# One product of each Strassen-Winograd projection split once more, and other places for the softmax weights

## The chip, the cores and the metric

The kernel runs on one core of one Trainium2 chip. The metric is the device time of one execution in microseconds, the median of several runs. Before the change it is 2482.03 us (three runs, 2481.46 to 2482.95).

A core has five engines, each with its own instruction queue that it works off in order: TensorE (PE; its weight loads are listed apart as PEld), VectorE (DVE), ScalarE (ACT), GpSimd (POOL) and SyncE (SP, which here issues the DMA transfers). They wait for each other through semaphores. Matmul results go to PSUM[...]; everything else lies in SBUF, 128 partitions wide.

## The reference

There are 128 graphs of 128 nodes with 512 features, float32, and two layers. Layer 0 reads them as batches, but its contractions are within one graph:

```
q, k, v = x @ Wq.T, x @ Wk.T, x @ Wv.T                  # layer 0
rel = adj.T * (q @ k.T);  rel = rel / norm(rel, rows)
x = layernorm(x + rel @ v)
q, k, v = x @ Wq + bq, x @ Wk + bk, x @ Wv + bv         # layer 1, 8 heads of 64
w = softmax(q @ k.T / 8 + mask(adj))                    # per head
x = layernorm(x + w @ v)
```

The kernel merges layer 0's two score weights into one matrix M (so y = x M stands for q and k together). That leaves five projections of 512 features to 512 features: m and v0 in layer 0, q, k and v1 in layer 1. They are most of the arithmetic.

## The kernel before, in words

**Tiling.** Four graphs make a group (512 tokens); there are 32 groups. Each projection of a group is a 512 x 512 by 512 x 512 product. It is done by one level of the Strassen-Winograd scheme: both operands are cut into quadrants of 256 x 256, and seven products P1 to P7 of quadrants, or of sums of quadrants, replace eight. The sums of the weights (`weight_sums`, tile `wc`) are made once, those of the tokens (`token_sums`, tiles `tx`) once a group, on VectorE and GpSimd. A product (`product`, L282) is four matmuls of 128 x 128 weights and 256 columns. A float32 matmul shows as two records, so a product shows as eight.

**A projection's course.** `Projection.step` takes the products in the order 1, 5, 6, 2, 3, 7, 4. P1, P6, P7 and P4 add up in one PSUM bank (`pa`), P5 and P3 in another (`pb`), P2 has one of its own (`pd`, from the pool `ps_m` of five banks that scores and outputs use too). ScalarE copies the running sums of P1, P5 and P6 out of the banks (`empty`, L290 or, with the bias, L293) into a tile `s`; VectorE adds the bank and one of these copies when P2, P3 and P7 are done (`add`, L297); ScalarE copies the last quadrant out after P4. A product that adds onto a bank waits until the copy before it has read that bank.

**The order of the work** is written out by hand. A round `r` has 35 slots. `dense` gives each slot one product; a projection starts every seven slots, and its P4 lies two slots inside the next projection. `short` holds all other steps, each with a slot number (halves allowed), in the tables `ZERO` (layer 0 of a group: scores, norm, outputs, layernorm, spill, staging, transposition), `STEADY`, `QUICK` and `LAST` (attention of layer 1). The loop at the end sorts the slots and issues what is in them; within an engine that is the order of execution. A slot number is no time: an instruction runs when its engine is free and its waits are over. In a steady round the projections are m and v0 of the next group, then q, k and v1 of this one.

**Other steps that are spoken of.** Layer 0's scores are `l0_score` (L334, 128-column matmuls; VectorE multiplies by the adjacency at L335, GpSimd squares at L336), its outputs `l0_out` (L379, L381). Layer 1's scores are `attn_scores` (L397, L401), then `attn_max`, `attn_exp` (ScalarE), a spill of the weights to DRAM and a staging back in an order that VectorE's 32 x 32 transposition needs, `attn_transpose`, `attn_out` (L450, L453), a way back through DRAM, and `attn_sum`, `attn_stats`, `attn_norm`. The last group has its own steps (`last_...`), without DRAM.

**Places.** SBUF tiles with one tag share a place in turn. Softmax weights `w` have two buffers of their own (tag "w"); layer 0's y and v have one place each ("yT", "v0"); the squares of layer 0 have one ("sq").

Of the kernel before, what the change touches and what calls it, by code (L numbers as in the profile page):

```python
# [18 lines left out]
def kernel(  # L19
# [15 lines left out]
    nc = tc.nc  # L35
# [101 lines left out]

    wc = {n: const.tile([P, 7, 2, HF], F32, name=f"wc_{n}") for n in ("m", "v0", "q", "k", "v1")}

    def weight_sums(t, a21, eng):  # L140
        eng.tensor_tensor(t[:, 4], a21, t[:, 3], op=ALU.add)
        eng.tensor_tensor(t[:, 5], t[:, 4], t[:, 0], op=ALU.subtract)
        eng.tensor_tensor(t[:, 6], t[:, 0], a21, op=ALU.subtract)
        eng.tensor_tensor(t[:, 2], t[:, 1], t[:, 5], op=ALU.subtract)
# [11 lines left out]
        return t.rearrange("p (q c r) -> p c q r", q=A, c=C)  # L156


    m21 = two.tile([P, 2, HF], F32, tag="w", name="m21")
    v21 = two.tile([P, 2, HF], F32, tag="w", name="v21")  # L160

    def layer0_weights():
        wq_p = one.tile([P, C, C, A, Q], F32, tag="v1", name="wq0_p")
# [24 lines left out]
        weight_sums(t, w[:, 0:2, HF:D], nc.gpsimd)  # L188


    XT, TX, YT, V0, REL, X1T, TX1, QT, KT, V1 = ({} for _ in range(10))
    SOFT = {}

    def transpose_quarter(dst, g, h, dh):
# [7 lines left out]
    def token_sums(t, xT, dh):  # L202

        if dh == 0:
            nc.vector.tensor_tensor(t[:, 0], quarter(xT, 0, 1), quarter(xT, 0, 0), op=ALU.subtract)
        else:
            nc.vector.tensor_tensor(t[:, 1], quarter(xT, 1, 1), t[:, 0], op=ALU.subtract)
            nc.gpsimd.tensor_tensor(t[:, 2], quarter(xT, 1, 1), quarter(xT, 0, 1), op=ALU.subtract)
            nc.gpsimd.tensor_tensor(t[:, 3], quarter(xT, 1, 0), t[:, 1], op=ALU.subtract)

    def x_transpose(g, dh, h):
        if dh == 0 and h == 0:
# [29 lines left out]
    class Projection:  # L242
# [7 lines left out]

        def begin(self):
            k, g = self.kind, self.g
            if k in ("m", "v0"):
                self.xT, self.t = XT[g], TX[g]
            else:
                self.xT, self.t = X1T[g], TX1[g]
            if k == "m":
                YT[g] = self.y = one.tile([P, C, G, P], F32, tag="yT", name=f"yT_{g}")
            elif k == "q":
                QT[g] = self.y = one.tile([P, C, G, P], F32, tag="qT" if g < NG - 1 else "yT", name=f"qT_{g}")  # L260
            elif k == "k":
                KT[g] = self.y = one.tile([P, C, G, P], F32, tag="kT", name=f"kT_{g}")
            elif k == "v0":
                V0[g] = self.y = one.tile([P, G, D], F32, tag="v0", name=f"v0_{g}")
            else:
                V1[g] = self.y = one.tile([P, G, D], F32, tag="v1" if g < NG - 1 else "v0", name=f"v1_{g}")
            self.s = one.tile([P, 3, 2, HF], F32, tag="s", name=f"s_{self.name}")

        def out(self, eh, th):
            if self.wide:  # L270
# [25 lines left out]
        def add(self, eh, th, bank, s):  # L296
            nc.vector.tensor_tensor(self.out(eh, th), bank, self.s[:, s], op=ALU.add)  # L297

        def step(self, i):
            if i == 1:  # L300
                self.begin()
                self.a = ps_a.tile([P, 2, HF], F32, tag="a", name=f"pa_{self.name}")
                self.product(1, self.a, True)
                self.empty(self.s[:, 0], self.a, 0)
            elif i == 5:
                self.b = ps_b.tile([P, 2, HF], F32, tag="b", name=f"pb_{self.name}")
                self.product(5, self.b, True)
                self.empty(self.s[:, 1], self.b, 1)
            elif i == 2:
                d = ps_m.tile([P, 2, HF], F32, tag="m", name=f"pd_{self.name}")  # L310
                self.product(2, d, True)
                self.add(0, 0, d, 0)
            elif i == 6:
                self.product(6, self.a, False)
                self.empty(self.s[:, 2], self.a, 0)
            elif i == 3:
                self.product(3, self.b, False)
                self.add(0, 1, self.b, 2)
            elif i == 7:
                self.product(7, self.a, False)  # L320
                self.add(1, 1, self.a, 1)
            elif i == 4:
                self.product(4, self.a, False)
                self.empty(self.out(1, 0), self.a, 1)

    def l0_score(g, b):

        if b == 0:
            REL[g] = (one.tile([P, G, P], F32, tag="rel", name=f"rel_{g}"),
                      one.tile([P, G, P], F32, tag="sq", name=f"sq_{g}"))  # L330
        rel, sq = REL[g]
        p = ps_m.tile([P, P], F32, tag="m", name=f"pst_{g}_{b}")
        for dc in range(C):
            nc.tensor.matmul(p, XT[g][:, dc, b, :], YT[g][:, dc, b, :], start=(dc == 0), stop=(dc == C - 1))  # L334
        nc.vector.tensor_tensor(rel[:, b], p, adj_sb, op=ALU.mult)  # L335
        nc.gpsimd.tensor_tensor(sq[:, b], rel[:, b], rel[:, b], op=ALU.mult)  # L336
# [51 lines left out]
    def l0_layernorm(g, b):  # L388
        normalized(graph(g, b), b, *RN[g])

    def attn_scores(g, b):

        p = [ps_m.tile([P, A, H // 2, Q], F32, tag="m", name=f"ps_{g}_{b}_{s}") for s in range(2)]
        for a in range(H // 2):
            for s in range(2):
                r = slice(s * HD, (s + 1) * HD)
                nc.tensor.matmul(p[s][:, :, a, :], QT[g][r, a, b, :], KT[g][r, a, b, :], start=True, stop=True)  # L397

        w = two.tile([P, 2, A, H // 2, Q], F32, tag="xl" if g == NG - 2 and b >= 2 else "w", name=f"w_{g}_{b}")
        for s in range(2):  # L400
            nc.vector.scalar_tensor_tensor(w[:, s].rearrange("p q a r -> p (q a r)"),  # L401
                                           p[s].rearrange("p q a r -> p (q a r)"), HD ** -0.5, mask,
                                           op0=ALU.mult, op1=ALU.add)
        nmax = small.tile([P, H], F32, tag="nmax", name=f"nmax_{g}_{b}")
        sums = small.tile([P, H], F32, tag="sums", name=f"sums_{g}_{b}")
        SOFT[g, b] = [w, nmax, sums]
# [97 lines left out]
    def last_scores(g, b):  # L504
        p = [ps_m.tile([P, H // 2, P], F32, tag="m", name=f"ps_{g}_{b}_{s}") for s in range(2)]
        for a in range(H // 2):
            for s in range(2):
                r = slice(s * HD, (s + 1) * HD)
                nc.tensor.matmul(p[s][:, a, :], QT[g][r, a, b, :], KT[g][r, a, b, :], start=True, stop=True)
        w = two.tile([P, H, P], F32, tag="w" if b < 2 else "xl", name=f"w_{g}_{b}")  # L510
        for s in range(2):
            nc.vector.scalar_tensor_tensor(w[:, s * (H // 2):(s + 1) * (H // 2)], p[s], HD ** -0.5,
                                           maskp[:, None, :].to_broadcast([P, H // 2, P]), op0=ALU.mult, op1=ALU.add)
# [57 lines left out]
    def last_store(g, b):  # L571
# [10 lines left out]

    ZERO = (
        ((18, 19, 20, 21), 22, (36, 36, 37, 37), 38, (39, 40), (40, 41), (42, 43), (46, 47, 49, 50)),
        ((10.5, 14, 10.5, 14), 15.5, (22, 22, 20.5, 18.5), 22.5, (24.5, 27), (32, 29.5), (33.5, 29.5), (36.5, 40.5, 41, 43.5)),
        ((11, 12, 13, 14), 16, (18, 19, 21, 22), 23, (24, 25), (25, 26), (26, 28), (31, 32, 33, 34)),
    )
    STEADY = (
        (32, (35.5, 35.5, 35.5, 35.5, 36), (35.5, 36), 39, (41.5, 51, 52, 53.5, 56.5, 59.5, 59.5, 61.5)),
        (32, (33.5, 37.5, 39, 41.5, 41.5), (42, 42), 42, (50, 51, 54.5, 60, 60.5, 63, 65.5, 72)),  # L590
        (51, (51.5, 51.5, 51.5, 53.5, 53.5), (52, 53.5), 56, (60, 67, 67, 68, 72, 74.5, 78, 78)),
        (51, (53, 54, 56, 56.5, 56.5), (56, 59), 61, (64.5, 67, 67.5, 74, 77, 81, 82, 84)),
    )
    QUICK = (
        (31.5, (32, 33.5, 34, 35, 35), (35, 37.5), 40.5, (44, 44, 44.5, 46.5, 50, 51.5, 51.5, 55)),
        (35.5, (36, 37, 37, 38, 38), (38, 41), 42.5, (44.5, 47.5, 48, 49.5, 52.5, 53.5, 58, 59.5)),
        (36, (39, 40, 41, 41, 41), (41.5, 42), 46, (49.5, 51.5, 51.5, 56.5, 56.5, 58.5, 61, 66.5)),
        (40.5, (41, 44, 45, 47, 47), (45, 49), 50, (54, 54.5, 59.5, 61, 62, 68, 68, 68)),
    )
    LAST = (  # L600
        (17, (17.5, 21.5), (22.5, 22.5), (24, 25), 29, 29, 29),
        (17.5, (18, 23), (24, 26.5), (28, 31), 36.5, 37, 37.5),
        (19, (23, 24.5), (27, 29.5), (31, 34.5), 41, 41, 42.5),
        (22.5, (25.5, 26), (29, 32), (34, 39), 41.5, 43.5, 47.5),
    )

    def at(r, k, f, *a):
# [2 lines left out]
    for r in range(-1, NG):  # L610
# [4 lines left out]
        for j, (kind, g) in enumerate(todo):  # L615
            if not 0 <= g < NG:
                continue
            pr = Projection(kind, g)
            for k, i in ((0, 1), (1, 5), (3, 6), (4, 2), (5, 3), (6, 7), (9, 4)):
                dense[R * r + 7 * j + k] = (pr, i)  # L620
    halves = [(dh, h) for dh in range(2) for h in range(2)]
    for g in range(NG):
# [11 lines left out]
        for i, (dh, h) in enumerate(halves):  # L634
            at(g - 2, ((24, 25, 27, 28) if g != 1 else (22, 23, 24, 25))[i], x_transpose, g, dh, h)
            at(g - 1, tr[i], x1_transpose, g, dh, h)
        for b in range(G):
            at(g - 1, sc[b], l0_score, g, b)
            at(g - 1, ou[b], l0_out, g, b)
# [29 lines left out]

    at(-1, 8, masks)  # L670
    at(-1, 41, layer1_weights, "k", "k")

    with tc.manual_schedule():
        layer0_weights()
# [39 lines left out]
```

## Time and profile before

| | |
|---|---|
| time, median of 3 | 2482.03 us |
| span of the profiled execution | 2480.6 us |
| TensorE busy | 2461.6 us |
| VectorE busy | 1603.6 us |
| ScalarE busy | 1012.8 us |
| GpSimd busy | 833.5 us |
| DMA moved | 404.73 MB |
| matmul records | 14656 |

Busy time is the sum of an engine's instructions without their overlaps. The durations of single records are from start to end; successive matmuls overlap, so what one costs is the distance between two starts. In a list of groups a row has the line, the engine, the operation, what it writes and reads with the shapes, how many there are, the busy time in us, the mean duration of one in ns, and the engine's idle time just before them with what ended it. In a list of waits a row has who waited for whom, the total in us, how often, and the longest.

### The profile page before, as it was taken

To read this page: it belongs to the slowest core of one execution; us is meant where nothing else is said; L and a number is where in the kernel's file an instruction comes from. 1 tells how busy PE (TensorE), PEld (TensorE's weight loads), DVE (VectorE), ACT (ScalarE), POOL (GpSimd) and SP (SyncE) were. 2 spreads that over 40 slices of the span, in tenths; PEclk is the share of its full clock that TensorE was granted. 3 is DMA by queue.
4 is the path that set the end of the run, shared out by engine and by line. 5 is a ranking of instruction groups with operands and counts; after the bars stand their busy time and mean duration, and the time that the engine had idled before them with its cause. 6 is when DMAs were issued, how large, how long until landed. Compare 5 with 4: busy or idle time off the path is not lost.

```text
span 2480.6 us, 41595 instructions
## 1 busy us (share of the span) xinstructions
PE 2461.6 (99%) x14656; PEld 2115.2 (85%) x14656; DVE 1603.6 (65%) x2715; ACT 1012.8 (41%) x3211; POOL 833.5 (34%) x1206
## 2 busy tenths in 40 slices
PE   8999999999999999999999999999999999999998
PEld 6888888888888888888888888888888888888886
DVE  5466676666666666666666666666666666666667
ACT  1243343433443433434334444434343344433454
POOL 3322333323323323233233233333332332323334
PEclk9999999999999999999999999999999999999999
DMA  7356656666555656556665556665566655665654
GB/s 158 102 132 166 179 154 166 169 164 170 173 159 160 176 164 183 156 160 169 169 170 170 157 160 175 162 183 159 162 171 164 174 166 157 165 175 159 182 149 141
DMA packets 508562, 404.73 MB, mean 163 GB/s; under 512 B 37569, under 2 KB 424769, under 8 KB 508353
## 3 DMA queue, kind: packets, MB, share of 16 engines
q1 hardware_dynamic: 508352, 402.08, 59.2%
q8 instruction: 114, 1.87, 0.3%
q14 instruction: 96, 0.78, 0.1%
HBM read 237.31 MB, written 164.63 MB: 162 GB/s over the span
## 4 chain that ended last, share of the span: by engine, by line
PE 98%; DVE 1%; issue 0%; DMA 0%; POOL 0%; POOLq 0%; ACT 0%; SPq 0%; DVEq 0%
PE pa_v L282 18%; PE pa_m L282 9%; PE pa_q L282 9%; PE pa_k L282 9%; PE pb_v L282 9%; PE ps L397 5%; PE po L450 5%; PE pd_v L282 5%; PE pst L334 5%; PE po L379 4%; PE pb_q L282 4%; PE pb_k L282 4%; PE pb_m L282 4%; PE pd_q L282 2%; PE pd_k L282 2%; PE pd_m L282 2%
## 5 line engine op out<-in xcount | busy, mean ns | idle before, releaser
L478 POOL TENSOR_TENSOR xr<-xr,bv_b 128x512 f32<-128x512 f32 x124 | 164.7, 1328 | 709.5 <-DMA xr<-x1d 300.6
L418 ACT ACTIVATE w<-w,nmax 128x128 f32<-128x128 f32 x992 | 384.8, 396 | 3.8 <-DVE nmax L411 3.8
L282 PE MATMUL pa_v<-wc_v,tx 128*128 128x256 f32 x1536 | 366.5, 382 | 0.0
L282 PEld LDWEIGHTS pa_v<-wc_v,tx 128*128 128x128 f32 x1536 | 289.6, 190 | 41.5 <-issue 0.6
L480 POOL TENSOR_TENSOR xr<-xr,o 128x512 f32<-128x512 f32 x124 | 157.4, 1269 | 288.6 <-issue 267.8
L418 ACT ACTIVATION_READ_ACCUMULATOR w<-w,nmax 128x1 f32 x992 | 193.6, 195 | 0.0
L282 PE MATMUL pa_m<-tx,wc_m 128*128 128x256 f32 x768 | 181.6, 380 | 0.8 <-DVE yT L297 0.8
L282 PE MATMUL pa_q<-tx,wc_q 128*128 128x256 f32 x768 | 181.7, 380 | 0.0
L282 PE MATMUL pa_k<-tx,wc_k 128*128 128x256 f32 x768 | 181.6, 380 | 0.0
L453 DVE STREAM_TRANSPOSE oT<-po 128x512 f32<-128x512 f32 x124 | 88.8, 716 | 141.2 <-PE po L450 139.9
L437 DVE STREAM_TRANSPOSE wT<-wl 128x1024 f32<-128x1024 f32 x124 | 153.8, 1240 | 30.2 <-DMA wl<-wd 30.2
L290 ACT COPY s_m<-pa_m 128x512 f32<-128x512 f32 x64 | 37.1, 580 | 330.6 <-PE pa_m L282 320.1
L290 ACT COPY s_v<-pa_v 128x512 f32<-128x512 f32 x128 | 74.9, 585 | 233.7 <-PE pa_v L282 233.7
L401 DVE SCALAR_TENSOR_TENSOR w<-ps,mask 128x512 f32<-128x512 f32 x248 | 154.2, 684 | 24.2 <-PE ps L397 24.2
L282 PEld LDWEIGHTS pa_m<-tx,wc_m 128*128 128x128 f32 x768 | 146.1, 190 | 21.1 <-DVE yT L297 1.2
L282 PEld LDWEIGHTS pa_k<-tx,wc_k 128*128 128x128 f32 x768 | 146.1, 190 | 19.7 <-issue 0.2
L282 PEld LDWEIGHTS pa_q<-tx,wc_q 128*128 128x128 f32 x768 | 146.0, 190 | 19.7 <-issue 0.2
L411 DVE TENSOR_REDUCE nmax<-w 128x4 f32<-128x512 f32 x248 | 154.8, 676 | 0.0
L374 ACT ACTIVATE xr<-xr,sh,rstd 128x512 f32<-128x512 f32 x124 | 100.8, 813 | 128.6 <-POOL sh L369 128.6
L196 DVE STREAM_TRANSPOSE x1T<-xl_h 128x512 f32<-128x512 f32 x128 | 90.1, 704 | 72.7 <-DMA xl_h<-x1d 72.7
L334 PEld LDWEIGHTS pst<-yT,xT 128*128 128x128 f32 x1024 | 124.7, 192 | 3.7 <-ACT yT L290 0.4
L397 PE MATMUL ps<-kT,qT 64*128 64x128 f32 x1984 | 127.7, 279 | 0.0
(160 smaller groups left out, 4905.6 us busy)
## 6 DMA issues: line engine op xcount, KB each, us to landing
wd<-w SPq DMA_DIRECT2D x248, 256.0 KB, 2.9
wl<-wd SPq DMA_DIRECT2D x496, 128.0 KB, 3.0
xl_x<-in_x_dram SPq DMA_DIRECT2D x256, 128.0 KB, 6.7
x<-in_x_dram SPq DMA_DIRECT2D x64, 512.0 KB, 5.6
x1d<-x SPq DMA_DIRECT2D x64, 512.0 KB, 2.9
xl_h<-x1d SPq DMA_DIRECT2D x256, 128.0 KB, 3.2
od<-oT SPq DMA_DIRECT2D x496, 64.0 KB, 1.9
o<-od SPq DMA_DIRECT2D x124, 256.0 KB, 3.1
```

What stands on the lines that cost most here:

```text
L282: nc.tensor.matmul(bank[:, m, :], l[:, k, m * P:(m + 1) * P], r[:, k, :], start=start and m == 0 and k == 0, stop=(m == 1 and k == 1), ski ...
L290: nc.scalar.copy(dst, bank)
L334: nc.tensor.matmul(p, XT[g][:, dc, b, :], YT[g][:, dc, b, :], start=(dc == 0), stop=(dc == C - 1))
L374: nc.scalar.activation(h, h, AF.Identity, bias=sh[:, b:b + 1], scale=rstd[:, b:b + 1])
L397: nc.tensor.matmul(p[s][:, :, a, :], QT[g][r, a, b, :], KT[g][r, a, b, :], start=True, stop=True)
L401: nc.vector.scalar_tensor_tensor(w[:, s].rearrange("p q a r -> p (q a r)"), p[s].rearrange("p q a r -> p (q a r)"), HD ** -0.5, mask, op0= ...
L411: nc.vector.tensor_reduce(nmax[:, s * (H // 2):(s + 1) * (H // 2)], w[:, s].rearrange("p q a r -> p a q r"), axis=AX.XY, op=ALU.max, negat ...
L418: nc.scalar.activation(w[:, s, :, a, :], w[:, s, :, a, :], AF.Exp, bias=nmax[:, i:i + 1], accum_out=sums[:, i:i + 1])
L437: nc.vector.transpose(wT, SOFT[g, b][0].rearrange("p a i r -> p i a r"))
L450: nc.tensor.matmul(p[s * HD:(s + 1) * HD, a, :], V1[g][:, b, h * HD:(h + 1) * HD], wT[:, s * (H // 2) + a].rearrange("p q t -> p (q t)"), ...
L478: nc.gpsimd.tensor_tensor(xr, xr, bv_b, op=ALU.add)
L480: nc.gpsimd.tensor_tensor(xr_, xr_, o, op=ALU.add)
```

## The change

P2 is the product of two plain quadrants of 256 x 256. The change applies the same scheme to it once more: seven products of 128 x 128 x 128 instead of four matmuls of 256 columns. Two quarters of P2's result need sums over several small products, and P2's result itself goes only to one quadrant of the output, onto P1's copy. The first group's m and v0 (`plain`) keep the old P2.

- New sums: of the weights once (`inner_weight_sums`, on GpSimd), of the tokens once a group and layer (`inner_token_sums`, on GpSimd, tiles `ux`).
- The small products come in four groups (`inner(0)` to `inner(3)`), placed by the table `INNER` between the products. They work in one bank of `ps_m` with three slots of 128 columns: three products, then two onto slots 0 and 1, then one onto slot 0, then one more onto slot 0. After each group VectorE adds the slots onto quarters of the output, which already hold P1's copy (`s0`). For v1, that copy lies in the place of layer 0's `rel`, and the output's place is taken later.
- The old P2 slot stays in the table, but is empty. So P3 follows P6.
- The memory for this comes from the softmax weights: a pair of them now lies in the place of layer 0's v or y, between uses. The squares lie in the place of `oT`.
- The tables ZERO, STEADY, QUICK and LAST have other slot numbers for many steps.

```diff
+    def inner_weight_sums(key, eng):
+        w = [None] + [inner_weight(key, i) for i in range(1, 8)]
+        eng.tensor_tensor(w[5], w[3], w[4], op=ALU.add)
+        eng.tensor_tensor(w[6], w[5], w[1], op=ALU.subtract)
+        eng.tensor_tensor(w[7], w[1], w[3], op=ALU.subtract)
+        eng.tensor_tensor(w[3], w[2], w[6], op=ALU.subtract)
...
+    def inner_token_sums(u, xT):
+
+        eng = nc.gpsimd
+        eng.tensor_tensor(u[:, 0], inner_token(xT, 5), inner_token(xT, 1), op=ALU.subtract)
+        eng.tensor_tensor(u[:, 1], inner_token(xT, 3), u[:, 0], op=ALU.subtract)
+        eng.tensor_tensor(u[:, 2], inner_token(xT, 3), inner_token(xT, 5), op=ALU.subtract)
+        eng.tensor_tensor(u[:, 3], inner_token(xT, 2), u[:, 1], op=ALU.subtract)
...
+        def inner_product(self, i, slot, start=False):
+            l, r = inner_weight(self.kind, i), self.u[:, {5: 0, 6: 1, 7: 2, 4: 3}[i]] if i >= 4 else inner_token(self.xT, i)
+        if self.wide:
+            l, r = r, l
+        nc.tensor.matmul(self.c[:, slot, :], l, r, start=start, stop=True, skip_group_check=True)
+
+        def inner(self, n):
+
+            add = nc.vector.tensor_tensor
+            self.u = (UX if self.kind in ("m", "v0") else UX1)[self.g]
+            if n == 0:
+                if self.kind == "v1":
+                    self.place()
+                self.c = ps_m.tile([P, 3, P], F32, tag="m", name=f"pc_{self.name}")
+                self.inner_product(1, 0, True)
+                self.inner_product(5, 1)
+                self.inner_product(2, 2)
+                y, s0 = self.quarters((1, 1))
+                add(y, self.c[:, 0:2], s0, op=ALU.add)
+                y, _ = self.quarters((0, 0))
+                add(y, self.c[:, 2], y, op=ALU.add)
+            elif n == 1:
+                self.inner_product(6, 0)
+                self.inner_product(3, 1)
+                y, s0 = self.quarters((0, 1))
+                add(y, self.c[:, 0], s0, op=ALU.add)
+                add(y, self.c[:, 1], y, op=ALU.add)
+            elif n == 2:
+                self.inner_product(7, 0)
+                y = self.last_quarter()
+                add(y, self.c[:, 0], y, op=ALU.add)
+            else:
+                self.inner_product(4, 0)
+                y, s0 = self.quarters((1, 0))
+                add(y, self.c[:, 0], s0, op=ALU.add)
...
             elif i == 2:
-                d = ps_m.tile([P, 2, HF], F32, tag="m", name=f"pd_{self.name}")
-                self.product(2, d, True)
-                self.add(0, 0, d, 0)
+                if self.plain:
+                    d = ps_m.tile([P, 2, HF], F32, tag="m", name=f"pd_{self.name}")
+                    self.product(2, d, True)
+                    nc.vector.tensor_tensor(self.s0, d, self.s0, op=ALU.add)
...
-                      one.tile([P, G, P], F32, tag="sq", name=f"sq_{g}"))
+                      two.tile([P, G, P], F32, tag="oT", name=f"sq_{g}"))
...
-        w = two.tile([P, 2, A, H // 2, Q], F32, tag="xl" if g == NG - 2 and b >= 2 else "w", name=f"w_{g}_{b}")
+        if g == NG - 2 and b >= 2:
+            w = two.tile([P, 2, A, H // 2, Q], F32, tag="xl", name=f"w_{g}_{b}")
+        else:
+            if b % 2 == 0:
+                WP[g, b // 2] = one.tile([P, 2, 2, A, H // 2, Q], F32, tag="yT" if b else "v0", name=f"w_{g}_{b}")
+            w = WP[g, b // 2][:, b % 2]
...
+    INNER = (
+        (2.71, 6.22, 8.23, 9.24),
+        (4.21, 8.72, 9.23, 9.74),
+        (2.21, 4.22, 6.73, 8.24),
+    )
...
-            for k, i in ((0, 1), (1, 5), (3, 6), (4, 2), (5, 3), (6, 7), (9, 4)):
+            for k, i in (*((0, 1), (1, 5), (3, 6), (4, 2), (5, 3), (6, 7), (9, 4)), *zip(INNER[2 if r == NG - 1 else kind == "v1"], range(10, 14))):
+                assert R * r + 7 * j + k not in dense
                 dense[R * r + 7 * j + k] = (pr, i)
```

The first row of `INNER` is for m, v0, q and k, the second for v1, the third for the last round. So, with the slots 0 (P1), 1 (P5), 3 (P6), 5 (P3), 6 (P7) and 9 (P4), and 7 and 8 for the next projection's P1 and P5, a projection other than v1 runs P1, P5, [the P4 before it], I0, P6, P3, P7, I1, next P1, next P5, I2, P4, I3; v1 has I0 ahead of P3, and I1, P4, I2, the next projection's I0, I3 at its end.

## The prediction

> **What bounds the kernel now.** I read the engines' busy time first, then the chain that ended last, then the waits of TensorE, and then its timeline.
>
> ```profile
> PE 2461.6 (99%) x14656; PEld 2115.2 (85%) x14656; DVE 1603.6 (65%) x2715; ACT 1012.8 (41%) x3211; POOL 833.5 (34%) x1206
> PEclk9999999999999999999999999999999999999999
> PE 98%; DVE 1%; issue 0%; DMA 0%; POOL 0%; POOLq 0%; ACT 0%; SPq 0%; DVEq 0%
> ```
>
> TensorE is busy for the whole span at full clock, and the chain is TensorE's own queue. Its waits add up to about 10 us, all in the first 55 us or the last 25:
>
> ```profile
> PE pM L177 <- DMA wk_s<-in_L_gnn_Wk_dram: 4.4, 1, 4.4
> PE po L546 <- DVE o L551: 1.8, 3, 1.2
> PE pa_m L282 <- DVE xT L196: 1.1, 1, 1.1
> PE pn L345 <- POOL sq L336: 0.9, 1, 0.9
> ```
>
> So between 55 and 2455 us a nanosecond off TensorE's queue is a nanosecond off the time, if no new wait appears; a nanosecond more on another engine costs nothing until TensorE waits for it. One steady round, from one pair of attention scores to the same pair of the next group, is 75.95 us, all TensorE (columns: length, PE, PEld, DVE, ACT, POOL, clock, DMA, GB/s):
>
> ```profile
> 1030.96:1106.91 75.95, 75.95 (x458) 65.57 (x458) 49.76 (x85) 31.47 (x100) 25.52 (x37) 1.00 0.61 167
> ```
>
> The prices of the two products stand side by side in TensorE's timeline:
>
> ```profile
> 1055.42 1.89 PE L282 MATMUL pa_v<-wc_v,tx 128*128 128x256 f32 x8
> 1057.15 1.95 PE L334 MATMUL pst<-yT,xT 128*128 128x128 f32 x16
> 1058.93 1.89 PE L282 MATMUL pd_v<-wc_v,xT 128*128 128x256 f32 x8
> 1060.66 1.89 PE L282 MATMUL pb_v<-wc_v,xT 128*128 128x256 f32 x8
> ```
>
> The reader should subtract starts, not read durations, which overlap. A product of L282 (four matmuls, eight records) takes 1058.93 to 1060.66, so 1.73 us, 0.216 a record. Sixteen records of 128 columns take 1057.15 to 1058.93, so 1.78 us, 0.111 a record, with the change of width into them and out of them included.
>
> **What the Trainium skill says.** "TensorE: Matmul & The Clock Gate", section "Wait — 56ns, not 53.3ns?": warm, matmuls follow each other at N/2.4 ns and about 2.5 ns more. The trace agrees if a float32 record streams its columns twice: 215.8 for 256 columns (0.216 here), 109.2 for 128 (0.111 here). The same page, "Step-by-step: what each phase is for", says that weight loads are pulled ahead of running matmuls. Here the 128-column loads of L334 have 190 to 193 ns each, yet records follow at 111, so they do overlap. "SBUF — State Buffer", "SBUF: two separate sides", says that a VectorE operation with two SBUF inputs and a GpSimd operation lock each other out. The added VectorE additions read one input from PSUM, so I don't count this; L297, of that kind, keeps its 691 ns.
>
> **The change part by part.** I call P2's seven small products by their groups: I0 (three products), I1 (two), I2 and I3 (one each).
>
> *TensorE.* Removed: P2, 1.726 us (eleven products from 1038.16 to 1057.15). Added: seven products of 128x128x128, two records each: 14 x 0.1113 = 1.558. Saved: 0.168 us a projection. There are 5 x 32 = 160 projections, and m and v0 of group 0 keep the old P2: 158 x 0.168 = **26.6 us**. The width changes cost nothing extra in the row above, even though the small products now come in groups of 6, 4, 2 and 2 records.
>
> *VectorE.* The kinds of operation, by their nearest rows:
>
> ```profile
> L335 DVE TENSOR_TENSOR rel<-pst,adj_sb 128x128 f32<-128x128 f32 x128 | 37.3, 292 | 98.2 <-PE pst L334 98.0
> L551 DVE TENSOR_TENSOR o<-po,rs 128x256 f32<-128x256 f32 x8 | 3.4, 425 | 2.0 <-PE po L546 1.3
> L297 DVE TENSOR_TENSOR v<-pd_v,s_v 128x512 f32<-128x512 f32 x64 | 44.2, 691 | 35.5 <-PE pd_v L282 35.5
> L336 POOL TENSOR_TENSOR sq<-rel 128x128 f32<-128x128 f32 x128 | 50.4, 398 | 152.5 <-DVE rel L335 151.7
> ```
>
> P2's addition (0.69) becomes one of 256 columns and five of 128: 0.425 + 5 x 0.292 = 1.89. That is 1.19 us more a projection, 158 x 1.19 = 188 us in all: VectorE goes from 1604 to about 1792 us, 73% of the new span; in a round 49.8 + 6.0 = 55.8 of about 75.1. It stays second. TensorE's products hide it, as long as each addition is done when its bank is written again.
>
> *GpSimd.* Four sums of 128 columns for each of 63 token tiles and five weights: 272 x 0.40 = 109 us, 833 to about 940, 38%. The token sums of a group are finished many products before their first use; hidden.
>
> *The new hand-offs.* I1, I2 and I3 reuse slot 0 of the bank and wait for the addition that read it; TensorE's whole queue stands behind such a wait. What one hand-off needs: the four-matmul score that starts at 1057.15 leaves the array after 8 x 0.111, at 1058.04, and its VectorE reader starts here:
>
> ```profile
> 1058.24 0.29 DVE L335 TENSOR_TENSOR rel<-pst,adj_sb 128x128 f32<-128x128 f32 x1 [1.44 <-PE pst L334]
> ```
>
> 0.20 to start, 0.29 for the addition, and 0.06 back (near the end L551 ends at 2460.27 and its waiter starts at 2460.33): 0.55 us, if VectorE is free. What lies between, from the slots: for m, v0, q and k, I1 to I2 has the next projection's P1 and P5 (3.45 us) and I2 to I3 has P4 (1.73): slack of 1.2 us or more, enough for one 1.15 us transposition in front. Laying VectorE's queue of a round against these places by the rows' durations, I find k the worst: some 3 us of backlog from transpositions and statistics before P3, and still I1's additions end 1.4 us before I2. For v1, I2 to I3 has only m's I0: six records, 0.67 us against 0.55. VectorE is idle there in this layout, so the wait is 0 to 0.1; it could be 0.6 if an operation of 512 columns got in front.
>
> *The other waits.* With P2 gone, only P3 (1.73 us) lies between P6 and P7, which writes P6's bank; before it was P2 and P3, 3.45. ScalarE needs 0.2 + 0.59 for a copy, or 0.2 + 0.84 for q's and k's two halves, and is 41% busy; four exps ahead of it (0.39 each, 1.55) would spoil it, but in q they are laid to end 1.8 us before P7 starts. Also, v0's bank is now held over the scores, so those work in four banks of the pool, not five; the last pair waits for the transposition of the output (0.64 after TensorE's end), which comes about level: 0 to 0.3. I take 0.1 us a round for these and v1 together: 31 x 0.1 = **3 us**; the bounds are 0 and 0.9 (28 us).
>
> *Softmax weights in the places of v and y.* No operation is added. Weights for graphs 0 and 1 lie in v's place from after its last reader until their spill; the next v writes graphs 2 and 3 some five products later. y's place is free from the last score (slot 11) to the next m (slot 35). A DMA read of some 3 us fits in both. Cost 0. The same goes for squares in oT.
>
> *Ends.* In the last 35 us VectorE, not TensorE, sets the pace: from 2442 to 2475 its operations stand nearly without a gap. The last v1's 1.19 us come on top: **+1.2**. At the start the first q may wait for its token sums, since four GpSimd sums follow the old ones: **+1**.
>
> Sum: 2482.0 - 26.6 + 3 + 1.2 + 1 = 2460.6; I say **2460**.
>
> **Rivals.** *A, nothing waits*: the bounds' low end, 2482 - 26.6 = 2455.4. For it: there is no steady wait now and every slack but one exceeds 0.5 us. Against: v1's 0.12 us. *B, hand-offs eat half*: v1's I3 and the fourth score bank late by some 0.45 us a round together, 14 us: 2471. For it: VectorE at 73% in strict order, where one late transfer (L196 waits 72.7 us for DMA now) holds up additions that TensorE now needs sooner. Against: those transfers get earlier places. *C, slower*: VectorE or ScalarE is late at every projection by more than the 0.168 saved; with 0.3 us each, 158 x (0.3 - 0.168) = +21, 2503. For it: three new TensorE waits a projection, 474 in all, and half the room before P7. Against: the round's VectorE sum, 55.8 of 75.1, and slack beyond 1 us at four of five. A version of C, where small matmuls can't hide their weight loads (14 x 0.19 = 2.66, +148 us), is refuted by the 0.111 of L334.
>
> **How the numbers follow.** Forecast 0.63, A 0.12, B 0.17, C 0.08, of which a part ends near no change. The low end takes in most of A; the high end reaches to B's value: 2454 to 2472. Faster by over 0.2% (under 2477): the forecast, A and B, 0.92; within it 0.03; slower 0.05.
>
> **What would show it.** Right: TensorE still at 98% or more, small products at 0.11 us a record, a round of about 75.2 us, VectorE near 1790, and waits of TensorE for VectorE of a few us in total. Wrong: a wait of TensorE for the additions of I2 or I1 some 31 or 158 times, or for ScalarE's copies before P7, or a gap at each change of width, which would bring the record over 0.111.

## The result and the profile after

The changed kernel takes 2458.86 us (median of 4 runs, 2458.22 to 2459.89), the kernel before 2481.79 beside it (2481.46 to 2482.95): ratio 0.9907, 95% interval 0.989 to 0.9924. The forecast was 2460, with a range of 2454 to 2472.

First the busy time, the clock and the chain on the page of the kernel after:

```profile
PE 2435.0 (99%) x15604; PEld 2123.7 (86%) x15604; DVE 1738.2 (71%) x3505; ACT 1000.4 (41%) x3211; POOL 952.3 (39%) x1478
PEclk9999999999999999999999999999999999999999
PE 98%; DVE 1%; POOL 0%; issue 0%; DMA 0%; POOLq 0%; ACT 0%; SPq 0%; DVEq 0%
```

TensorE has 948 records more and is busy 26.6 us less (2461.6 before). That this is the forecast's saving to the tenth is chance: up to 3.4 us of it come from two stretches of the trace of before that ran at half the granted clock (see the last section). The chain is still TensorE's own queue. Of its waits, these are the two longest and the two for the split product (total, times, longest):

```profile
PE pM L193 <- DMA wk_s<-in_L_gnn_Wk_dram: 4.4, 1, 4.4
PE po L557 <- DVE wT L544: 1.5, 1, 1.5
PE pc_v L360 <- DVE v L386: 0.6, 1, 0.6
PE pc_m L360 <- POOL ux L234: 0.5, 1, 0.5
```

The list has eleven rows. Ten waits occur once and one twice, all of them in the first 62 us or the last 35; no wait is repeated from round to round. The two for the split product (line 360) lie at the two ends of the kernel.

From one start of m to the next, a steady round is 75.20 us, before 75.96. Twenty-nine such rounds take 2181.11 us in this trace and 2202.71 in that of before: 21.6 of the 24.3 us between the two profiled spans. The rest is the start (2.65) and the end (0.1).

Now the tightest place of the prediction, v1's I2 and I3 with only m's I0 between. TensorE's timeline of the kernel after:

```profile
1030.51 1.89 PE L327 MATMUL pa_v<-wc_v,tx 128*128 128x256 f32 x8
1032.24 0.39 PE L360 MATMUL pc_v<-wd_v,ux 128*128 128x128 f32 x2
1032.46 0.39 PE L360 MATMUL pc_m<-xT,wc_m 128*128 128x128 f32 x2
1032.68 0.39 PE L360 MATMUL pc_m<-ux,wd_m 128*128 128x128 f32 x2
1032.91 0.39 PE L360 MATMUL pc_m<-xT,wc_m 128*128 128x128 f32 x2
1033.13 0.39 PE L360 MATMUL pc_v<-wc_v,ux 128*128 128x128 f32 x2
1033.35 1.89 PE L327 MATMUL pa_m<-tx,wc_m 128*128 128x256 f32 x8
```

and VectorE's there:

```profile
1031.04 0.29 DVE L382 TENSOR_TENSOR v<-pc_v,v 128x128 f32<-128x128 f32 x1
1032.66 0.29 DVE L386 TENSOR_TENSOR v<-pc_v,v 128x128 f32<-128x128 f32 x1 [1.33 <-PE pc_v L360]
```

Subtract starts: every small product takes 0.22 us (two records), a large one 1.73. I2 has had its turn on TensorE at 1032.46, VectorE has been idle for 1.33 us, adds from 1032.66 to 1032.95, and I3 starts at 1033.13 without a gap. That is 0.18 us after the addition; with 0.06 for the way back, 0.12 us were to spare, as forecast.

The one small loss that does repeat is the fourth score bank. A steady round has two pairs of scores, here with what follows each:

```profile
1056.82 2.12 PE L499 MATMUL ps<-kT,qT 64*128 64x128 f32 x32
1058.87 1.99 PE L327 MATMUL pa_q<-x1T,wc_q 128*128 128x256 f32 x8
1095.60 2.06 PE L499 MATMUL ps<-kT,qT 64*128 64x128 f32 x32
1097.58 0.49 PE L360 MATMUL pc_v<-wc_v,x1T 128*128 128x128 f32 x2
```

The first pair takes 1058.87 - 1056.82 = 2.05 us, the second 1097.58 - 1095.60 = 1.98, as both do in the trace of before. Within the first, the weight load for the last bank starts only at 1057.78, behind the transposition of the output that frees this bank at 1057.73:

```profile
1057.01 0.72 DVE L560 STREAM_TRANSPOSE oT<-po 128x512 f32<-128x512 f32 x1
```

So 0.06 to 0.07 us a round are lost, some 2 us in all. No other loss repeats: a large product takes 1.73 us to the next start, except beside scores or other matmuls of another shape (1.82 or 1.83, in before too), so ScalarE's copies hold nothing up.

### The profile page after: what moved, and what is told of

The parts are those of the page before. It is cut to its first block, busy times and chain, and to the rows that moved or that the text cites. A ratio compares the mean times of both kernels' runs of the same rounds, so it can differ in the third digit from the quotient of the medians.

```text
span 2456.3 us, 44484 instructions
## 1 busy us (share of the span) xinstructions
PE 2435.0 (99%) x15604; PEld 2123.7 (86%) x15604; DVE 1738.2 (71%) x3505; ACT 1000.4 (41%) x3211; POOL 952.3 (39%) x1478
## 4 chain that ended last, share of the span: by engine, by line
PE 98%; DVE 1%; POOL 0%; issue 0%; DMA 0%; POOLq 0%; ACT 0%; SPq 0%; DVEq 0%
PE pa_v L327 18%; PE pa_q L327 9%; PE pa_k L327 9%; PE pa_m L327 9%; PE pb_v L327 9%; PE ps L499 5%; PE po L557 5%; PE pst L434 5%; PE pb_q L327 5%; PE pb_k L327 4%; PE pb_m L327 4%; PE po L479 4%; PE pc_v L360 4%; PE pc_q L360 2%; PE pc_k L360 2%; PE pc_m L360 2%
## 5 line engine op out<-in xcount | busy, mean ns | idle before, releaser
L585 POOL TENSOR_TENSOR xr<-xr,bv_b 128x512 f32<-128x512 f32 x124 | 158.4, 1278 | 626.0 <-DMA xr<-x1d 204.8
L327 PEld LDWEIGHTS pa_v<-wc_v,tx 128*128 128x128 f32 x1536 | 282.1, 190 | 33.7
L338 ACT ACTIVATE qT<-pa_q,bq_sb 128x256 f32<-128x256 f32 x128 | 53.6, 470 | 271.9 <-PE pa_q L327 271.9
L327 PEld LDWEIGHTS pa_m<-tx,wc_m 128*128 128x128 f32 x768 | 141.1, 190 | 17.8 <-DVE yT L342 1.2
L327 PEld LDWEIGHTS pa_k<-tx,wc_k 128*128 128x128 f32 x768 | 141.0, 190 | 16.6 <-issue 0.2
L335 ACT COPY yT<-pa_m 128x512 f32<-128x512 f32 x64 | 37.7, 590 | 231.2 <-PE pa_m L327 231.2
L499 PEld LDWEIGHTS ps<-kT,qT 64*128 64x128 f32 x1984 | 117.4, 187 | 11.2 <-issue 10.8
L479 PE MATMUL po<-v,rel 128*128 128x512 f32 x256 | 125.4, 592 | 0.0
```

What stands on the lines that cost most here:

```text
L327: nc.tensor.matmul(bank[:, m, :], l[:, k, m * P:(m + 1) * P], r[:, k, :], start=start and m == 0 and k == 0, stop=(m == 1 and k == 1), ski ...
L479: nc.tensor.matmul(p, REL[g][0][:, b, :], V0[g][:, b, :], start=True, stop=True)
L585: nc.gpsimd.tensor_tensor(xr, xr, bv_b, op=ALU.add)
```

## The experiments

All times are medians, each beside runs of the kernel before (medians of 2481.5 to 2481.8); every kernel is the one after with the edit shown.

| kernel | us | ratio to before (95%) | steady round, us |
|---|---|---|---|
| after | 2458.86 | 0.9907 (0.989 to 0.9924) | 75.20 |
| e1_old_p2 | 2483.46 | 1.0006 (0.9997 to 1.0015) | 76.00 |
| e2_old_tables | 2519.31 | 1.0149 (1.0134 to 1.0164) | 76.6 (mean) |
| e3_v1_no_gap | 2479.39 | 0.9991 (0.9982 to 0.9999) | 75.85 |
| e5_double_adds | 2476.70 | 0.9981 (0.9973 to 0.9989) | 75.72 |
| e6_old_but_x1 | 2482.79 | 1.0002 (0.9994 to 1.0011) | 75.65 (mean) |
| e7_x1_back | 2492.92 | 1.0045 (1.0028 to 1.0062) | 76.36 (mean) |
| e8_old_last | 2460.94 | 0.9917 (0.9902 to 0.9932) | 75.20 |
| e4_no_gap | 2541.35 | 1.0241 (1.0226 to 1.0257) | 77.85 |

### e1: the old P2 in the new tables and places

```diff
-            self.plain = x0 and g == 0
+            self.plain = True
...
-                    nc.vector.tensor_tensor(self.s0, d, self.s0, op=ALU.add)
+                    if self.kind == "v1":
+                        self.place()
+                    nc.vector.tensor_tensor(self.out(0, 0), d, self.s0, op=ALU.add)
```

The sums are still made. Those of the weights overwrite a quarter that the old P2 reads, so this kernel does not compute the reference's result; TensorE and VectorE have the instructions of before.

> The changed kernel with the old P2 (four matmuls of 256 columns) in all 160 projections; new slot tables, new places, all sums for the small products still made on GpSimd but unused. Pitch theory (the gain is TensorE's record count times its pitch, nothing else): back to the time before, 2480 to 2485 us, TensorE a bit over 2460 busy, VectorE near 1600. Rival, the new tables and places bring part of the gain: 2475 or less. Rival, the new tables need the shorter P2 stage or lose by themselves: over 2487.

Measured: 2483.46 us. The page of this kernel:

```profile
PE 2459.0 (99%) x14656; PEld 2110.4 (85%) x14656; DVE 1597.7 (64%) x2715; ACT 1003.6 (40%) x3211; POOL 953.4 (38%) x1478
```

The number of records is that of before, and the time too to within 2 us, though GpSimd makes all the sums. New tables, new places and sums bring nothing by themselves and cost at most these 2 us. The gain is P2's pitch, the distance between the starts of its records times their number.

### e2: the split P2 in the old tables

ZERO, STEADY, QUICK and LAST as before the change. The row that turned out to matter:

```diff
-        ((10.5, 10.5, 10.5, 11), 13.5, (22.5, 21.5, 20, 19.5), 24, (28.5, 27), (31, 30.5), (35, 32.5), (38, 40.5, 42.5, 44.5)),
+        ((10.5, 14, 10.5, 14), 15.5, (22, 22, 20.5, 18.5), 22.5, (24.5, 27), (32, 29.5), (33.5, 29.5), (36.5, 40.5, 41, 43.5)),
```

> The changed kernel with the small products and new places, but the four slot tables as they were before. Pitch theory: 2457 to 2465, since additions have slack over 1 us at four projections of five wherever the other steps lie; a few us more where a VectorE step of 1.2 us happens to fall in v1's short gap. Rival, the additions are only in time because of the new tables: over 2475, with TensorE waiting for VectorE or ScalarE 31 times or more.

Measured: 2519.31 us, 60 more than after and 1.5% more than before. My theory missed; the rival had it right. TensorE's largest wait in this kernel, and then one of VectorE's:

```profile
PE pc_v L360 <- DVE v L382: 31.2, 29, 2.1
```

```profile
DVE x1T L212 <- DMA xl_h<-x1d: 87.0, 26, 4.4
```

TensorE waits once a round, at v1's I2, for I1's second addition. VectorE itself waits for layer 1's input (x1) to come back from DRAM. The kernel before had that wait too (72.7 us at L196), and TensorE did not wait in its steady rounds; the reading is that nothing it needed soon stood behind the transposition there. In the old tables the first x1 transposition stands at slot 36.5 (1.5 of the next round), just ahead of v1's I1 additions (1.72). That is the new theory, tried from both sides in e6 and e7.

### e7: only that chain's start moved back in the new tables

The three entries of the first half of x1 (its spill, its staging and its first transposition) have their old slots.

```diff
-        ((10.5, 10.5, 10.5, 11), 13.5, (22.5, 21.5, 20, 19.5), 24, (28.5, 27), (31, 30.5), (35, 32.5), (38, 40.5, 42.5, 44.5)),
+        ((10.5, 10.5, 10.5, 11), 13.5, (22.5, 21.5, 20, 19.5), 24, (28.5, 27), (32, 30.5), (33.5, 32.5), (36.5, 40.5, 42.5, 44.5)),
```

> The kernel after with only the start of that chain moved back: spill at slot 32, staging at 33.5, first transposition at 36.5 (1.5 of the next round), which puts it ahead of v1's I1 additions in VectorE's queue. Theory: this alone brings the wait of TensorE back at v1's I2, 0.6 to 1.2 us and 0.3 of restarts a round over 30 rounds: 2484 to 2504 us. Rival (other entries cause it): 2457 to 2462, VectorE waits for the DMA with nothing urgent behind it.

Measured: 2492.92 us, 34 more than after, as the theory had it. One round on VectorE's timeline in this kernel:

```profile
1196.96 0.71 DVE L212 STREAM_TRANSPOSE x1T<-xl_h 128x512 f32<-128x512 f32 x1 [3.32 <-DMA xl_h<-x1d]
1197.59 0.25 DVE L381 TENSOR_TENSOR v<-pc_v,s_v 128x128 f32<-128x128 f32 x1
1197.88 0.29 DVE L382 TENSOR_TENSOR v<-pc_v,v 128x128 f32<-128x128 f32 x1
```

and on TensorE's:

```profile
1195.01 0.38 PE L360 MATMUL pc_v<-wd_v,ux 128*128 128x128 f32 x2
1195.23 0.39 PE L360 MATMUL pc_v<-wc_v,x1T 128*128 128x128 f32 x2
1195.45 1.89 PE L327 MATMUL pa_v<-wc_v,tx 128*128 128x256 f32 x8
1198.23 0.49 PE L360 MATMUL pc_v<-wd_v,ux 128*128 128x128 f32 x2 [0.88 <-DVE v L382]
```

I1's products are through at 1195.45. VectorE was free from 1193.64, but its next instruction is the transposition, whose data come only at 1196.96. The two additions behind it (0.29 us each) end at 1198.17 instead of about 1196.3 (0.20 after I1, then as in the timeline of after), and TensorE, whose P4 is done at 1197.18, stands until 1198.23: 1.05 us, and 0.10 more until the next product (1198.55 instead of 1198.45). Added up from the starts of records, 31.8 of the 33.4 us that the 29 steady rounds lose against after lie at this place.

### e6: the old tables, with only that chain placed as in the new ones

```diff
-        ((10.5, 14, 10.5, 14), 15.5, (22, 22, 20.5, 18.5), 22.5, (24.5, 27), (32, 29.5), (33.5, 29.5), (36.5, 40.5, 41, 43.5)),
+        ((10.5, 14, 10.5, 14), 15.5, (22, 22, 20.5, 18.5), 22.5, (24.5, 27), (31, 30.5), (35, 32.5), (38, 40.5, 42.5, 44.5)),
```

(against e2's tables; here the entries of both halves of x1 move)

> The kernel after with the tables ZERO, STEADY, QUICK and LAST of before, except for one row's three entries: layer 1's input (x1) is spilled, staged and transposed at the new slots (first transposition at slot 38 instead of 36.5). Theory: with all old tables 2519 us came out because VectorE, in strict order, stood at this transposition waiting for its DMA while v1's I1 additions stood behind it; TensorE then waited 1.2 us at v1's I2. Moving it behind I3 should take that wait away: a round of 75.2 to 75.4 us, and 2472 to 2486 us in all, what is left over the kernel after being the end (13.6 us in the trace with all old tables) and the start (1.8). Rival: the wait comes from other old entries (scores, maxima, sums in VectorE's queue): then a round stays at 76 or more and the time at 2505 to 2520.

Measured: 2482.79 us, 36.5 less than e2, inside the theory's 2472 to 2486; the mean round of 75.65 is a little over the expected 75.4. VectorE's and TensorE's waits in this kernel:

```profile
DVE x1T L212 <- DMA xl_h<-x1d: 1.9, 4, 0.5
```

```profile
PE pc_m L360 <- DVE yT L386: 5.2, 11, 1.0
PE ps L499 <- DVE oT L560: 3.6, 1, 3.6
PE po L557 <- DVE wT L544: 3.4, 2, 1.8
```

The wait at v1's I2 is gone. What remains of e2's loss in the rounds is again additions that come late behind other VectorE work: against after, 8.4 us are lost at m's I3, where an x1 transposition (L212) stands ahead of the addition, and 4.3 us at k's I3, which is 0.15 us late in every round behind sums of tokens (L223). The end is 10.5 us longer than after's, up to 3.4 of it from a stretch at half the granted clock. Which old entries are behind these was not tried.

### e3 and e4: what a bare hand-off costs

e3 puts v1's I3 right behind I2; e4 does it for m, v0, q and k.

```diff
-        (4.21, 8.72, 9.23, 9.74),
+        (4.21, 8.72, 9.23, 9.24),
```

```diff
-        (2.71, 6.22, 8.23, 9.24),
+        (2.71, 6.22, 8.23, 8.24),
```

> The changed kernel with v1's last small product (I3) issued right behind the one before it (I2), ahead of m's I0 and not after it. Hand-off theory: each of some 31 waits exposes 0.20 to start, 0.29 for the addition and 0.06 back, 0.55 us, plus up to 0.1 for a weight load that isn't hidden: 17 to 20 us, so 2476 to 2479, and a wait of TensorE for VectorE's addition on L386 of about that sum. Rival, VectorE is behind at that place: over 2485. Rival, the wait is hidden or the gap of 0.67 was never needed: under 2465.

> The kernel after with I3 of m, v0, q and k right behind I2, with no product between (their P4 then comes after both); v1 as it was. Each then has a bare hand-off: TensorE stands for I2's end, its addition and the way back, 0.55 us, and 0.10 for the restart, as v1 showed. Theory: 124 x 0.65 = 81 us more, 2535 to 2545 us. Rival: VectorE often has a transposition of 1.15 us or statistics in front at these places, so the wait is longer by half of such an operation on average: 2555 to 2600.

Measured: 2479.39 us (e3, 20.5 over after) and 2541.35 (e4, 82.5 over). e3 lies 0.4 over the upper end of its theory, e4 inside; all rivals are out. The longest waits of TensorE in e4:

```profile
PE pc_m L360 <- DVE yT L386: 13.3, 28, 0.5
PE pc_v L360 <- DVE v L386: 12.4, 32, 0.6
PE pc_q L360 <- DVE qT L386: 12.0, 31, 0.5
PE pc_k L360 <- DVE kT L386: 11.9, 31, 0.4
```

They sum to some 50 us, but the loss is 82.5: a wait as listed is less than the gap in the queue. One of v0's on TensorE's and VectorE's timelines in e4:

```profile
1020.69 0.38 PE L360 MATMUL pc_v<-wd_v,ux 128*128 128x128 f32 x2
1021.46 0.49 PE L360 MATMUL pc_v<-wc_v,ux 128*128 128x128 f32 x2 [0.38 <-DVE v L386]
1021.78 1.89 PE L327 MATMUL pa_v<-wc_v,tx 128*128 128x256 f32 x8
```

```profile
1021.11 0.29 DVE L386 TENSOR_TENSOR v<-pc_v,v 128x128 f32<-128x128 f32 x1 [2.35 <-PE pc_v L360]
```

Start to start: I2's two records end their turn at 1020.69 + 0.22 = 1020.91; the addition starts 0.20 later, takes 0.29, and I3 starts 0.06 after its end. That is 0.55 us, the prediction's sum to the hundredth. Then I3 itself takes 0.32 to the next start instead of 0.22: 0.10 more after a standstill. 0.65 us x 124 = 81. e3's rounds show the same two parts, 0.55 and 0.10.

### e5: each addition made twice

A second addition of 128 columns into a spare tile stands behind each of the six.

```diff
+    junk = const.tile([P, P], F32, name="junk")
...
-            add = nc.vector.tensor_tensor
+            def add(y, c, s, op):
+                nc.vector.tensor_tensor(y, c, s, op=op)
+                if len(c.shape) == 3:
+                    c, s = c[:, 0], s[:, 0]
+                nc.vector.tensor_tensor(junk, c, s, op=op)
```

> The changed kernel with one more addition of 128 columns behind each of the six additions of a projection's small products, written to a spare tile: 158 x 6 x 0.29 = 277 us more for VectorE, to about 2015 us (82%). Pitch theory with the slack as laid out: only v1's I2 to I3 (0.67 us) must now hold 0.20 + 0.29 and, ahead of it, nothing new, while I1's spare additions lie in P4's 1.73 us: 0 to 0.3 us a round there, and some 0.1 to 0.3 at the scores' fourth bank: 2459 to 2475. Rival, VectorE is close to setting the time: over 2490, waits spread over all projections.

Measured: 2476.70 us, 1.7 over the upper end. The page of this kernel:

```profile
PE 2450.7 (99%) x15604; PEld 2124.1 (86%) x15604; DVE 1983.2 (80%) x4453; ACT 1003.5 (41%) x3211; POOL 953.8 (39%) x1478
```

VectorE works 245 us more for 948 additions (0.258 each), and the time grows by 17.8. In the trace some 15 us are lost in the steady rounds and 2.2 at the end. A round loses 0.52 us at two places only: 0.20 in front of v1's I3 and 0.10 behind it, 0.12 in front of k's I2 and 0.10 behind it. k is where the prediction had found VectorE's longest backlog:

```profile
1095.90 1.89 PE L328 MATMUL pb_v<-wc_v,tx 128*128 128x256 f32 x8
1097.74 0.49 PE L361 MATMUL pc_k<-ux,wd_k 128*128 128x128 f32 x2
```

```profile
1097.40 0.29 DVE L369 TENSOR_TENSOR junk<-pc_k,kT 128x128 f32<-128x128 f32 x1
```

The product in front of I2 takes 1097.74 - 1095.90 = 1.84 us to the next start and not 1.73, since the last spare addition ends at 1097.69. So 93% of the added VectorE work still lies beside TensorE; the loss is local, at two of the places with the least slack, not a matter of VectorE's share.

### e8: the last group's table as before

```diff
-        (17, (17.5, 17.5), (21.5, 21.5), (24, 24.5), 29, 31.5, 32),
+        (17, (17.5, 21.5), (22.5, 22.5), (24, 25), 29, 29, 29),
...
```

> The kernel after with the table LAST of before, that is with the last group's attention in its old order. The prediction added 1.2 us at the end for the last v1's additions on VectorE, which did not show. Theory: the new order of the end paid for it, so with the old order it shows: 2460 to 2462 us. Rival 1: the additions lie beside other waits and cost nothing in either order: 2458 to 2459.5. Rival 2: the old order of the end is what cost 13.6 us with all old tables: 2468 to 2474.

Measured: 2460.94 us (2459.83 to 2461.36), 2.1 over after, whose four runs reach up to 2459.89. The last v1's I3 in e8:

```profile
2431.85 0.49 PE L360 MATMUL pc_v<-wc_v,ux 128*128 128x128 f32 x2 [2.51 <-DVE v L386]
```

and in the kernel after:

```profile
2430.92 0.49 PE L360 MATMUL pc_v<-wc_v,ux 128*128 128x128 f32 x2 [0.56 <-DVE v L386]
```

The wait for the addition is 2.51 us in the old order and 0.56 in the new. Measured from the last start of m, the end is 151.81 us in e8, 151.15 after and 151.24 before. I3 itself starts 125.8 us after that m in both: the new order does not bring it forward, but lets other work of TensorE, scores (L616) and a transposition of weights (L638), run ahead of it. Only 0.66 us of the difference between the two traces comes from the end; the start, where the two kernels have the same order, differs by 1.36 (see the last section). The direction is as the theory had it, but its +1.2 is not confirmed in size.

## Why the prediction was right

TensorE's queue bounds the kernel after as it did the one before, and the saving is the one that was worked out from the distances between starts. With the sizes that the traces show, the sum is -25.8 + 1.9 + 0.8 - 0.1 = -23.2 us (saving, score bank, start, end), beside the 22.9 between the medians. One thing was luck: rival B stayed away, but not for the reason that was given.

- **TensorE's saving, -26.6**: right. In the trace the 158 split P2s take 158 x 14 x 0.1117 = 247.1 us, the old ones took 158 x 8 x 0.2159 = 272.9: 25.8 saved. The width changes cost nothing, as read from the scores of layer 0; e1 shows that nothing else of the change brings time. The 215.8 and 109.2 ns of the prediction are estimates with the columns counted twice; a record took 215.9 and 111.7. That it streams its columns twice was not tried by any run.
- **Hand-offs and score bank, +3**: right in mechanism, near in size: about 2 us, all of it the score bank (0.06 a round). The additions of I1 to I3 cost nothing in the steady rounds, and neither do the copies ahead of P7. The hand-off of 0.55 us was right to the hundredth (e3, e4), but the prediction left out that a wait costs 0.10 beyond its length.
- **Bounds of that term, 0 to 28**: with v1 bare it is 20.5 (e3), with the x1 transposition in the way 34 (e7). The second lies outside: I let an operation of 512 columns get in front of an addition, not one that itself waits for a transfer.
- **Rival B** named the right danger, the late x1 transfer ahead of the additions, but the reason against it was wrong. "Those transfers get earlier places" is true only of the spill (slot 32 to 31). The staging moves later (33.5 to 35) and the transposition too (36.5 to 38), behind v1's I3. VectorE hardly waits any more (72.7 us before, 2.9 after) since it comes for the data later. With the old place the price would have been 34 us, not B's 14. The forecast was lucky here: the change had moved the entries that matter, and the prediction had read the move the wrong way round.
- **The tables** got no price of their own. Without the split they are worth nothing (e1, which also bears out the cost of 0 for the softmax weights in v's and y's places); with it they are worth 60 us (e2).
- **VectorE, 1792 us**: 1738. The durations were right: the small additions last 281 to 292 ns, and summed they come to 184 us more than P2's additions in e1 (188 forecast). But busy time counts overlaps once. In this trace the instruction behind a small addition of 0.29 us often starts 0.21 us after it, before it ends; the second addition of I0 and of I1, which needs the first's result, starts 0.03 after the first's end. I added durations where the prediction itself had warned against that for TensorE. Nothing hung on it.
- **GpSimd, about 940 us**: 952; its sums of 128 columns took 455 ns where the row used had 398. Hidden, as said, but for the wait at the start.
- **End, +1.2**: 0.7 of it is there. From e1 to after, both with the new tables and at full clock up to the last matmul, the end grows from 150.43 to 151.15 us. Against before (151.24) it doesn't show: the new order of the last group saves 0.7 (e8), and before's end has 3.4 us at half the granted clock, whose share of the time was not measured.
- **Start, +1**: a wait for the token sums of about that size came, at m of the second group, not at the first q: TensorE stood for GpSimd's sums there (listed as 0.5 us; from start to start 0.7, and 0.1 behind it). Yet the start is 2.65 us shorter than before's: up to the third m the split saves 1.7 us of records, and before's trace has 1.7 us from a stretch at half the clock; see below.

## What to carry to other kernels

Splitting a product pays by the distance between starts (here 0.112 us a record of 128 columns against 0.216 of 256), provided that beside every hand-off of a reused bank TensorE has as much other work as the hand-off takes: here 0.55 us, and 0.65 is lost if there is none. A new dependence makes old, harmless waits expensive: look in the reading engine's queue for what stands ahead of the new instruction, above all an instruction that waits for a transfer. An engine's share of busy time says little of it: 80% cost 18 us in e5, 70% in e7 cost 34.

## What the runs showed of the hardware

- A wait of TensorE for VectorE costs about 0.10 us beyond its length: the next record takes 0.32 instead of 0.22, in e3, e4, e5 and e7 alike. The weight loads (PEld) show what may be behind it. The first line is I3 of v0 in e4, after its wait, the second v1's I3 in the kernel after, without one:

```profile
1021.46 0.30 PEld L360 LDWEIGHTS pc_v<-wc_v,ux 128*128 128x128 f32 x2 [0.57 <-DVE v L386]
1033.02 0.30 PEld L360 LDWEIGHTS pc_v<-wc_v,ux 128*128 128x128 f32 x2
```

  Without a wait the load starts 0.11 us ahead of its matmul (1033.13), under the record before. With one it starts when the wait is over, together with the matmul (1021.46). A load that is no longer hidden would explain the 0.10; no run tried it.
- In the traces of before, e2, e3, e5 and e8 the granted clock of TensorE falls to half for 3.41 us, soon after waits of 0.9 and 1.1 us, the second of which ends at about 53 us. In those of after, e1, e4, e6 and e7 it stays at full there, with the same waits, although after, e3 and e8 have the same order of work up to that point. Here before, then after (columns: stretch, length, busy time of PE, PEld, DVE, ACT and POOL, granted clock, DMA share, GB/s):

```profile
54.04:57.45 3.41, 3.41 (x8) 2.02 (x7) 2.14 (x4) 0.59 (x1) 1.88 (x2) 0.50 0.00 0
54.04:57.45 3.41, 3.41 (x14) 2.25 (x13) 3.34 (x6) 0.58 (x1) 1.93 (x2) 1.00 0.01 2
```

  The product behind the wait and the output after it take 5.24 us there in before and 3.55 in after, 1.7 us more. Such stretches also lie near the end in before (from 2460.44 us), e2 and e6, and in e7 at 1581 us. Why they come in one run and not in another stays open. In the profiled runs this fell in favour of the kernel after. The medians, 22.9 us apart, are therefore the better measure of the change than the spans of the two traces, 24.3 apart.
